# One convolution tap moved from VectorE to ScalarE and GpSimd, and the quarters of a block inverse stored by chunk in PSUM

## The chip, the cores and the metric

The kernel runs on one core of one Trainium2 chip. The metric is the device time of that core in microseconds (us); lower is better. The core has a matrix engine (TensorE, "PE" in the profile; its weight loads are "PEld"), a vector engine (VectorE, "DVE"), an engine for activations (ScalarE, "ACT"), a general engine (GpSimd, "POOL") and one that issues most of the DMAs (SyncE, "SP"). Each runs its own instruction stream in order and waits for the others by semaphores. Operands lie in SBUF; matmul results lie in PSUM.

## The reference, cut to what matters

A decoder of two layers on 16 sequences of 256 tokens of width 256. The change lies in the attention of layer 1, a gated delta rule with 16 query heads and 4 key/value heads of 128:

```python
x = x + _L0_attn_ref(_layernorm(x), ...)      # softmax attention
x = x + _L0_ffn_ref(_layernorm(x), ...)       # mixture of 8 experts
x = x + _L1_attn_ref(_layernorm(x), ...)      # below
x = x + _L1_ffn_ref(_layernorm(x), ...)       # gated MLP

def _L1_attn_ref(x, qkv_w, g_w, b_w, gk_w, conv_w, out_norm_w, o_w):
    qkv = x @ qkv_w.T
    y = sum(conv_w[:, i] * xp[:, i:i + S, :] for i in range(4))   # causal, per channel; xp: qkv, 3 zeros ahead
    qkv = silu(y)
    q, k, v = split(qkv)                     # q, k scaled to unit length
    alpha = exp(log_sigmoid(x @ gk_w.T) / 16); beta = sigmoid(x @ b_w.T)
    def step(St, inp):
        q_t, k_t, v_t, a_t, b_t = inp
        St = St * a_t
        delta = (v_t - k_t @ St) * b_t
        St = St + outer(k_t, delta)
        return St, q_t @ St
    o = scan(step, 0, ...)
    o = rmsnorm(o) * out_norm_w * silu(x @ g_w.T)
    return o @ o_w.T
```

The kernel does the recurrence in chunks of 128 tokens: inside a chunk it needs the inverse of a triangular 128x128 matrix (identity plus a strictly triangular part) for each head.

## The kernel before, in words

Three phases follow one another: layer 0 (attention and experts), attention 1 (the function `gated_delta`), and the last MLP (`ffn`). In attention 1 a **step** is one group of 4 query heads with its key/value head (j) on 512 tokens (s), that is two sequences; there are 4 x 8 = 32 steps. A **unit** is one sequence of a step, two chunks (c = 0, 1) of 128 tokens for 4 heads; there are 64 units. Four generators make the work, and `weave` interleaves them by fixed due times; a scheduler then sets each engine's order ahead of the run.

- `project`, once a step, for six tiles (k, v and four q): six matmuls into a PSUM bank (L902), then the convolution. ScalarE writes the tap without a shift into `acc` (L913). VectorE adds the other three, each a scalar_tensor_tensor that reads the PSUM bank shifted by d and `acc` (L917). ScalarE applies silu (L926), and for q a square (L929) whose sums TensorE makes (L951).
- `decays`, once a unit: for each chunk a DMA brings decays, repeated over all partitions, into `Dm` (L978); VectorE runs a scan over it (L984) with `bI`, which GpSimd makes (L982). `Dm0` has 4 buffers, `Dm1` 5. They stay in use until `back` has read them (o0, L1157, for chunk 0; o1, L1175, for chunk 1).
- `front`, once a unit, makes the inverse. GpSimd fills `XT` with a scaled identity (L996) and makes the triangular matrix `Tf` (L1008), which is split in two fp16 parts `Th` and `Tl`. VectorE puts the first off-diagonal entries into `XT` with copy_predicated (L1013) and transposes (L1019). Then the blocks double: at each of five levels (2, 4, 8, 16, 32) TensorE makes Y from `Th` and `X` (L1027), ScalarE copies it (L1029), TensorE makes Z from `XT` and Y (L1033), and VectorE copies Z under a mask into `X` (L1035) and transposes `X` to `XT` (L1041). The two chunks of `X` alternate element by element, and before the change so do those of Z in its bank.
- `back`, once a unit, solves with the inverse for both chunks (`solve`, z at L1110), carries the state `S0` (L1154), scales the output `O` (L1123, after a power on GpSimd, L88), gates it (L1131, L1133, L1134) and adds the projected rows to x (L1141, L1143).

The loads of `Dm`, of the activations `xT` and of the next weights all go through SP's queue, in order.

Of the kernel before, what the change touches and what calls it, by code (L numbers as in the profile page):

```python
# [10 lines left out]
F32 = mybir.dt.float32  # L11
I32 = mybir.dt.int32
U8 = mybir.dt.uint8
# [4 lines left out]
ALU = mybir.AluOpType  # L18
# [4 lines left out]
P = 128  # L23
# [11 lines left out]
G = H1 // KV1  # L35
LEVELS = (2, 4, 8, 16, 32)
XS = 2.0**12
WS, NS, OS, HS = 2.0**13, 2.0**10, 20.0, 0.5
PS0_BUFS = {"s": 3, "m": 3, "e": 1, "y": 1}
PS0_ROLE = {"s": "s", "t": "s", "p": "m", "n": "s", "v": "m", "o": "m", "r": "s", "e": "e", "y": "y", "l": "m", "g": "m"}  # L40
# [812 lines left out]
def gated_delta(tc, ctx, a, x, ident, identh, ones, psum, made, ws, weights, rsqrt_):  # L853
# [36 lines left out]
    DVE.tensor_scalar(nident, ident, -XS, None, ALU.mult)  # L890
    masks = p.tile([P, 512], F32, tag="Tf", name="masks", bufs=2)[:, :384].rearrange("p (n e) -> p n e", n=6)
    nc.sync.dma_start(out=masks, in_=a["blocks"])
    masks8 = wp.tile([P, 6, 64, 2], U8, tag="masks8", name="masks8")
    for c in range(2):
        DVE.tensor_copy(masks8[:, :, :, c], masks)
    pair1, odd = masks8[:, 0], {s: masks8[:, n + 1] for n, s in enumerate(LEVELS)}
    def three(ps, w, wcols, xs, xcols, flip=False):

        todo = [(c, m, n) for c in range(2) for m, n in ((0, 0), (0, 1), (1, 0))]
# [4 lines left out]
    def project(s, j, xT, w, r):  # L904

        nm = f"{s}_{j}"
        eq = p.tile([P, 4, G], F32, tag="eq", name=f"eq_{nm}", bufs=3)
        raw, tags = {}, cycle(("pr", "bk") if s == j == 0 else ("pr",))
        for n, ct in (("k", G), ("v", G + 1)) + tuple((h, h) for h in range(G)):
            ps = bank(f"pr_{nm}_{n}", next(tags))  # L910
            three(ps, w["wqkv"], slice(ct * P, (ct + 1) * P), xT, slice(0, 512))
            acc = p.tile([P, 512], F32, tag="acc", name=f"acc_{nm}_{n}", bufs=2)
            ACT.activation(acc, ps, AF.Copy, scale=w["cv"][:, ct, 3:4])  # L913
            to, frm = acc.rearrange("p (b t) -> p b t", b=2), ps.rearrange("p (b t) -> p b t", b=2)
            yield
            for d in (1, 2, 3):
                DVE.scalar_tensor_tensor(to[:, :, d:], frm[:, :, : S - d], w["cv"][:, ct, 3 - d : 4 - d], to[:, :, d:], ALU.mult, ALU.add)  # L917
                yield
            if n in ("k", "v"):
                raw[n] = dst = acc  # L920
            else:
                if n == 0:
                    q = p.tile([P, G, 512], F32, tag="q", name=f"q_{nm}")
                    r.update(q=q)
                dst = q[:, n, :]
            ACT.activation(dst, acc, AF.Silu)  # L926
            if n not in ("k", "v"):
                q2 = p.tile([P, 512], F32, tag="q2", name=f"q2_{nm}_{n}", bufs=1)
                ACT.activation(q2, dst, AF.Square)  # L929
            yield  # L930
            if n == "k":

                pk = bank(f"pk_{nm}", "pr").rearrange("p (i d) -> p i d", i=4)
                for i in range(4):
                    PE.transpose(pk[:, i, :], raw["k"][:, i * P : (i + 1) * P], ident)
                ss = p.tile([P, 4], F32, tag="kss", name=f"kss_{nm}")
                k2 = p.tile([P, P], F32, tag="sq", name=f"k2_{nm}", bufs=1)
                for i in range(4):
                    ACT.activation(k2, pk[:, i, :], AF.Square, accum_out=ss[:, i : i + 1])
                DVE.tensor_scalar(ss, ss, 1e-6, None, ALU.add)  # L940
                rsqrt_(ss, 4)
                k = p.tile([P, 4, P], F32, tag="k", name=f"k_{nm}")
                for i in range(4):
                    ACT.activation(k[:, i, :], pk[:, i, :], AF.Copy, scale=ss[:, i : i + 1])
                r.update(k=k)
                yield
            elif n != "v":

                pq = bank(f"pq_{nm}_{n}", "pr")[:, :4]
                for i in range(4):  # L950
                    PE.matmul(pq[:, i : i + 1], lhsT=q2[:, i * P : (i + 1) * P], rhs=ones[:, 0:1], start=True, stop=True)  # L951
                DVE.tensor_scalar(eq[:, :, n], pq, 1e-6, w["sv"][:, 1:2], ALU.add, ALU.mult)  # L952
                yield
            else:
                pv = bank(f"pv_{nm}", "pr")
                for i in range(4):
                    PE.transpose(pv[:, i * P : (i + 1) * P], raw["v"][:, i * P : (i + 1) * P], ident)
                v = p.tile([P, 4, P], F32, tag="v", name=f"v_{nm}", bufs=3)
                ACT.activation(v.rearrange("p i d -> p (i d)"), pv, AF.Copy, scale=w["sv"][:, 0:1])  # L959
                vh = p.tile([P, 2, P], F16, tag="vh", name=f"vh_{nm}", bufs=3)  # L960
                DVE.tensor_copy(vh, v.rearrange("p (b c) d -> p b c d", c=2)[:, :, 0, :])
                pt = bank(f"kn_{nm}", "pr")
                for i in range(4):
                    PE.transpose(pt[:, i * P : (i + 1) * P], r["k"][:, i, :], ident)
                kT = p.tile([P, 512], F32, tag="kT", name=f"kT_{nm}")
                ACT.copy(kT, pt)
                r.update(v=v, vh=vh, kT=kT)
                yield
        r.update(eq=eq)
        yield  # L970

    def decays(s, j, b, r):


        nm, hs = f"{s}_{j}_{b}", slice(G * j, G * j + G)
        Dm = [p.tile([P, G, P], F32, tag=f"Dm{c}", name=f"Dm{c}_{nm}", bufs=4 + c) for c in range(2)]
        for c in range(2):
            nc.sync.dma_start(out=Dm[c], in_=bcast(al_d[4 * s + 2 * b + c, hs, :], 0, P))  # L978
        yield
        for c in range(2):  # L980
            bI = p.tile([P, G, P], F32, tag="bI", name=f"bI_{nm}_{c}")
            POOL.tensor_tensor(bI, bcast(ident, 1, G), bcast(beta[:, 4 * s + 2 * b + c, hs], 2, P), ALU.mult)  # L982
            flat = lambda t: t.rearrange("p h t -> p (h t)")
            DVE.tensor_tensor_scan(flat(Dm[c]), flat(Dm[c]), flat(bI), 0.0, ALU.mult, ALU.add)  # L984
            yield
        end = p.tile([P, G], F32, tag="end", name=f"end_{nm}", bufs=5)
        DVE.tensor_copy(end, Dm[0][:, :, P - 1])
        r.update(A=Dm, end=end)
        yield

    def front(s, j, b, pr, r):
# [1 line left out]

        nm, A = f"{s}_{j}_{b}", r["A"]
        XT = p.tile([P, G, P, 2], F16, tag="XT", name=f"XT_{nm}", bufs=4)
        POOL.tensor_copy(XT.rearrange("p h t c -> p h (t c)").bitcast(I32), bcast(x0.rearrange("p t c -> p (t c)").bitcast(I32), 1, G))  # L996
        cols = lambda c: slice((2 * b + c) * P, (2 * b + c + 1) * P)
        pk = bank(f"kk_{nm}", "fr")[:, : 2 * P].rearrange("p (c t) -> p c t", c=2)
        for c in range(2):
# [10 lines left out]
            POOL.tensor_tensor(Tl[c], Tf, Th[c], ALU.subtract)  # L1010
            yield
        for c in range(2):
            DVE.copy_predicated(  # L1013
                XT.rearrange("p h (n two) c -> p h n two c", two=2)[:, :, :, 1, c], bcast(pair1[:, :, 0], 1, G),
                Th[c].rearrange("p h (n two) -> p h n two", two=2)[:, :, :, 1],
            )
        X = p.tile([P, G, P, 2], F16, tag="X", name=f"X_{nm}")
        words = lambda t: t.rearrange("p h t c -> p (h t c)").bitcast(F32)
        DVE.transpose(words(X), words(XT))  # L1019
# [1 line left out]
        for s_ in LEVELS:  # L1021
            even = lambda t: t.rearrange("p h (n two e) c -> p h n two e c", two=2, e=s_)[:, :, :, 0]
            py = bank(f"Y_{nm}_{s_}", "fr").rearrange("p (c h n) -> p c h n", c=2, h=G)
            pz = bank(f"Z_{nm}_{s_}", "fr").rearrange("p (h n c) -> p h n c", c=2, h=G)
            for c in range(2):
                for h in range(G):
                    PE.matmul(py[:, c, h, :], lhsT=Th[c][:, h, :], rhs=even(X)[:, h, :, :, c], start=True, stop=True)  # L1027
# [2 lines left out]
            yield  # L1030
            for c in range(2):
                for h in range(G):
                    PE.matmul(pz[:, h, :, c], lhsT=XT[:, h, :, c], rhs=Y[:, c, h, :], start=True, stop=True)  # L1033
            split = lambda t: t.rearrange("p h (n e) c -> p h n (e c)", e=s_)
            DVE.copy_predicated(  # L1035
                even(X).rearrange("p h n e c -> p h n (e c)"),
                bcast(odd[s_].rearrange("p (n e) c -> p n (e c)", e=s_), 1, G), split(pz),
            )
            yield
            if s_ < 32:  # L1040
# [31 lines left out]
    def back(s, j, b, pr, xT, w, r):  # L1072
# [20 lines left out]
        def solve(c, rh, rf):  # L1093
# [12 lines left out]
            yield  # L1106
            dz = ps(f"dz{c}")
            per_head(lambda h: PE.matmul(dz[:, h, :], lhsT=XF[:, c, h, :], rhs=res[:, h, :], start=True, stop=True))
            z = half(f"z{c}")
            DVE.scalar_tensor_tensor(z, dz, 1.0 / XS, zh, ALU.mult, ALU.add)  # L1110
            yield
            return z
# [4 lines left out]
        def finish(c, o):  # L1117

            per_head(lambda h: ACT.activation(sq, o[:, h, :], AF.Square, accum_out=f[:, c, h : h + 1]))
            DVE.scalar_tensor_tensor(f[:, c], f[:, c], 1.0 / DK, pr["eq"][:, 2 * b + c, :], ALU.mult, ALU.add)  # L1120
            rsqrt_(f[:, c], G)
            O = half(f"O{c}")
            per_head(lambda h: ACT.activation(O[:, h, :], o[:, h, :], AF.Copy, scale=f[:, c, h : h + 1]))  # L1123
            yield
            return O
# [24 lines left out]
        z0 = yield from solve(0, lambda h: pr["vh"][:, b, :], bcast(v[:, 2 * b, :], 1, G))  # L1150
        st = ps("st")
        per_head(lambda h: PE.matmul(st[:, h, :], lhsT=kb[:, h, :], rhs=z0[:, h, :], start=True, stop=True))
        S0 = half("S0", bufs=2)
        ACT.copy(S0, st)  # L1154
        yield
        o0 = ps("o0")
# [144 lines left out]
```

## Time and profile before

| | us |
|---|---|
| median of 3 runs (3420.18 to 3423.67) | 3420.84 |
| the profiled execution, its time | 3428.7 |
| the profiled execution, its span | 3426.8 |
| attention 1 within the span, about | 1170 to 3195 |

| engine | busy, us | share of the span |
|---|---|---|
| PE | 2963.0 | 86% |
| PEld | 2358.8 | 69% |
| DVE | 2580.1 | 75% |
| ACT | 2157.1 | 63% |
| POOL | 1891.2 | 55% |

The page of the profile has these parts: busy time of each engine; the same in 40 slices of the span; DMA queues; the chain of waits that ended last, followed back from the last instruction; groups of instructions by line (busy us, mean ns of one, then the idle time of the engine just before them and what ended it). Further answers of the trace give one line's instructions (least, median and greatest duration), who waited for whom, busy times in a stretch, and the instructions in order of time. "L917" is line 917 of the kernel before. Ends of matmuls in the trace are modelled, so what one matmul occupies is read from the start of the next.

### The profile page before, as it was taken

Reading aid. Unit: us, or ns where it says so; the run is one execution under the profiler, and the core shown is the slowest. Engines: PE = TensorE matmul, PEld = TensorE weight load, DVE = VectorE, ACT = ScalarE, POOL = GpSimd, SP = SyncE. Lnnn points to the kernel's source line nnn. Section 1 sums busy time; section 2 is a strip of 40 time slices with the busy share of each in tenths; the row PEclk is TensorE's granted clock in tenths of the full one; section 3 lists DMA queues with packets and bytes.
Section 4 is the critical chain, followed back from the end, with each engine's and each line's share of the span. In section 5 each row is a group of like instructions: output and inputs, shape, how many; then the busy total and the mean of one; then the engine's idle time right before and its main releaser. Section 6 shows DMA issues by size and latency. Waiting matters only on the chain.

```text
span 3426.8 us, 76022 instructions
## 1 busy us (share of the span) xinstructions
PE 2963.0 (86%) x29836; PEld 2358.8 (69%) x29836; DVE 2580.1 (75%) x4957; ACT 2157.1 (63%) x5327; POOL 1891.2 (55%) x1763
## 2 busy tenths in 40 slices
PE   4487997988788579899999989999899999999799
PEld 3365775766666357777777777777777777777588
DVE  4677787777775578888788888888888888886422
ACT  2466676666666457767676676766676767676432
POOL 2476876766667445555555555554555555554332
PEclk7699998999999779999999999999999999999899
DMA  6422332322321301211111111111111111110100
GB/s 183 144 77 62 95 86 78 101 73 79 80 52 43 78 16 37 60 46 42 32 35 56 44 44 41 35 38 50 48 50 32 38 33 40 35 35 8 32 19 25
DMA packets 175461, 188.70 MB, mean 55 GB/s; under 512 B 20494, under 2 KB 132878, under 8 KB 173374
## 3 DMA queue, kind: packets, MB, share of 16 engines
q1 hardware_dynamic: 165742, 167.07, 17.5%
q10 hardware_dynamic: 9360, 16.79, 1.6%
q8 instruction: 233, 3.82, 0.5%
q14 instruction: 126, 1.03, 0.1%
HBM read 150.14 MB, written 32.02 MB: 53 GB/s over the span
## 4 chain that ended last, share of the span: by engine, by line
PE 34%; DVE 20%; DMA 5%; ACT 5%; issue 2%; POOL 2%; SPq 0%; ACTq 0%; DVEq 0%; POOLq 0%
PE pr L902 5%; DMA Dm<-al_d 5%; DVE acc L917 3%; PE pq L951 3%; PE g L902 3%; DVE Dm L984 3%; DVE X L1035 2%; PE Z L1033 2%; PE fy L829 2%; PE fg L119 2%; PE fu L119 2%; DVE XT L1013 2%; PE Y L1027 2%; PE y L1141 2%; DVE XT L1041 1%
## 5 line engine op out<-in xcount | busy, mean ns | idle before, releaser
L547 POOL TENSOR_TENSOR el<-e,eh 128x512 f16<-128x512 f32 x384 | 444.9, 1170 | 159.7 <-ACT eh L546 122.1
L917 DVE SCALAR_TENSOR_TENSOR acc<-pr,cv,acc 128x510 f32<-128x510 f32 (+2 forms) x384 | 281.4, 734 | 73.7 <-ACT acc L913 69.7
L1008 POOL TENSOR_TENSOR Tf<-Dm,kkm 128x512 f32<-128x512 f32 x128 | 161.7, 1282 | 251.5 <-DVE kkm L1002 243.3
L543 ACT ACTIVATE e<-t 128x512 f32<-128x512 f32 x384 | 232.4, 606 | 105.0 <-PE t L541 67.5
L1035 DVE CAST_PREDICATED X<-masks,Z 128x512 f16<-128x512 uint8 x320 | 220.7, 690 | 70.8 <-PE Z L1033 70.6
L1134 POOL TENSOR_TENSOR gl<-sg,gh 128x512 f16<-128x512 f32 x128 | 158.0, 1235 | 156.3 <-ACT gh L1133 156.0
L546 ACT ACTIVATE eh<-t 128x512 f16<-128x512 f32 x384 | 232.0, 606 | 13.0 <-PE po L558 12.8
L1029 ACT ACTIVATE Y<-Y 128x512 f16<-128x512 f32 x320 | 191.2, 597 | 74.8 <-PE Y L1027 73.5
L984 DVE TENSOR_TENSOR_SCAN Dm<-Dm,bI 128x512 f32<-128x512 f32 x128 | 182.1, 1423 | 62.4 <-DMA Dm<-al_d 60.3
L1033 PE MATMUL Z<-Y,XT 128*128 128x64 f16 x2560 | 207.4, 249 | 23.6 <-ACT Y L1029 18.8
L88 POOL TENSOR_TENSOR f<-f,neghalf 128x4 f32<-128x4 f32 x128 | 149.2, 1166 | 124.9 <-DVE f L1120 122.7
L1033 PEld LDWEIGHTS <-XT 128*128 128x128 f16 x2560 | 175.3, 121 | 53.9 <-issue 31.8
L902 PE MATMUL pr<-xT,wqkv 128*128 128x512 f16 x768 | 209.3, 413 | 2.9 <-ACT v L959 2.8
L982 POOL TENSOR_TENSOR bI<-ident,beta 128x512 f32<-128x512 f32 x128 | 134.1, 1048 | 136.2 <-DVE Dm L984 98.3
L510 DVE TENSOR_REDUCE nm<-s 128x2 f32<-128x512 f32 x256 | 173.1, 682 | 47.3 <-PE s L509 46.4
L902 PEld LDWEIGHTS <-wqkv 128*128 128x128 f16 x1152 | 119.0, 112 | 120.7 <-issue 38.4
L902 PE MATMUL g<-xT,wga 128*128 128x256 f16 x1536 | 198.9, 281 | 1.4 <-DVE eq L952 0.7
L1141 PE MATMUL y<-woa,gh 128*128 128x256 f16 x1024 | 184.7, 277 | 7.7 <-ACT gh L1133 5.5
L1027 PE MATMUL Y<-X,Th 128*128 128x64 f16 x2560 | 145.5, 202 | 43.4 <-DVE X L1035 34.0
L1041 DVE STREAM_TRANSPOSE XT<-X 128x512 f32<-128x512 f32 x256 | 179.8, 702 | 1.9
L539 PE MATMUL t<-Qt,Kt 128*128 128x512 bf16 x384 | 152.2, 402 | 32.3 <-ACT eh L546 15.2
L1027 PEld LDWEIGHTS <-Th 128*128 128x128 f16 x2560 | 125.4, 101 | 67.2 <-issue 57.9
(363 smaller groups left out, 9829.3 us busy)
## 6 DMA issues: line engine op xcount, KB each, us to landing
Dm<-al_d SPq DMA_DIRECT2D x128, 256.0 KB
cb<-cd SPq DMA_DIRECT2D x128, 128.0 KB
dB<-dc_d ACTq DMA_DIRECT2D x64, 256.0 KB
xT<-xd SPq DMA_DIRECT2D x64, 256.0 KB
Qt<-qd SPq DMA_DIRECT2D x32, 408.0 KB
qd<-both SPq DMA_DIRECT2D x32, 192.0 KB
xr_gidx<-ix_gidx SPq DMA_DIRECT2D x34, 160.0 KB
xr_uidx<-ix_uidx SPq DMA_DIRECT2D x34, 160.0 KB
```

The lines of the kernel that those rows point to most:

```text
L543: ACT.activation(e32, ps, AF.Exp, scale=SC0)
L546: ACT.activation(eh[n], ps, AF.Exp, scale=SC0)
L547: POOL.tensor_tensor(el[n], e32, eh[n], ALU.subtract)
L902: PE.matmul(ps, lhsT=r if flip else l, rhs=l if flip else r, start=k == 0, stop=k == len(todo) - 1)
L917: DVE.scalar_tensor_tensor(to[:, :, d:], frm[:, :, : S - d], w["cv"][:, ct, 3 - d : 4 - d], to[:, :, d:], ALU.mult, ALU.add)
L984: DVE.tensor_tensor_scan(flat(Dm[c]), flat(Dm[c]), flat(bI), 0.0, ALU.mult, ALU.add)
L1027: PE.matmul(py[:, c, h, :], lhsT=Th[c][:, h, :], rhs=even(X)[:, h, :, :, c], start=True, stop=True)
L1029: ACT.activation(Y, py, AF.Copy, scale=XS**-2)
L1033: PE.matmul(pz[:, h, :, c], lhsT=XT[:, h, :, c], rhs=Y[:, c, h, :], start=True, stop=True)
L1035: DVE.copy_predicated(even(X).rearrange("p h n e c -> p h n (e c)"), bcast(odd[s_].rearrange("p (n e) c -> p n (e c)", e=s_), 1, G), split ...
L1041: DVE.transpose(words(XT), words(X))
L1141: PE.matmul(py, lhsT=pair[m][:, h, :], rhs=w["wo"][n][:, h, :], start=k == 0, stop=k == len(todo) - 1)
```

## The change

Of the convolution's three shifted taps, the one with d = 1 is no longer added by VectorE: ScalarE writes it, unshifted, into a new tile `tap` (one buffer), and GpSimd adds it with the shift, as the last of the taps. Z is laid out by chunk in its PSUM bank (each chunk's 256 values side by side), the masks are stored by head and no longer by chunk, and the masked copy reads the two chunks from the two halves of the bank. The first off-diagonal entries are put into `XT` by a scalar_tensor_tensor with a constant `pairs` instead of a copy_predicated with a mask, and GpSimd's fill of `XT` writes only the even columns (256 words instead of 512). `Dm0` gets 5 buffers and `Dm1` 6. Of `back`'s tiles, `z` and `O` share one buffer for both chunks, and `S0` has one buffer instead of two.

```diff
+SMALL = 2.0**-40
...
-    masks8 = wp.tile([P, 6, 64, 2], U8, tag="masks8", name="masks8")
-    for c in range(2):
-        DVE.tensor_copy(masks8[:, :, :, c], masks)
-    pair1, odd = masks8[:, 0], {s: masks8[:, n + 1] for n, s in enumerate(LEVELS)}
+    masks8 = wp.tile([P, 5, G, 64], U8, tag="masks8", name="masks8")
+    DVE.tensor_copy(masks8, bcast(masks[:, 1:], 2, G))
+
+    pairs = wp.tile([P, 64], F32, tag="pairs", name="pairs")
+    DVE.scalar_tensor_tensor(pairs, ident.rearrange("p (e two) -> p e two", two=2)[:, :, 1], XS / SMALL, masks[:, 0], ALU.mult, ALU.add)
+    odd = {s: masks8[:, n] for n, s in enumerate(LEVELS)}
...
             ACT.activation(acc, ps, AF.Copy, scale=w["cv"][:, ct, 3:4])
-            to, frm = acc.rearrange("p (b t) -> p b t", b=2), ps.rearrange("p (b t) -> p b t", b=2)
-            yield
-            for d in (1, 2, 3):
+            tap = p.tile([P, 512], F32, tag="tap", name=f"tap_{nm}_{n}", bufs=1)
+            ACT.activation(tap, ps, AF.Copy, scale=w["cv"][:, ct, 2:3])
+            to, frm, late = (t.rearrange("p (b t) -> p b t", b=2) for t in (acc, ps, tap))
+            yield
+            for d in (2, 3):
                 DVE.scalar_tensor_tensor(to[:, :, d:], frm[:, :, : S - d], w["cv"][:, ct, 3 - d : 4 - d], to[:, :, d:], ALU.mult, ALU.add)
                 yield
+            POOL.tensor_tensor(to[:, :, 1:], to[:, :, 1:], late[:, :, : S - 1], ALU.add)
+            yield
...
-        Dm = [p.tile([P, G, P], F32, tag=f"Dm{c}", name=f"Dm{c}_{nm}", bufs=4 + c) for c in range(2)]
+        Dm = [p.tile([P, G, P], F32, tag=f"Dm{c}", name=f"Dm{c}_{nm}", bufs=5 + c) for c in range(2)]
...
-        POOL.tensor_copy(XT.rearrange("p h t c -> p h (t c)").bitcast(I32), bcast(x0.rearrange("p t c -> p (t c)").bitcast(I32), 1, G))
+        even_cols = lambda t: t.bitcast(I32).rearrange("p (m two) -> p m two", two=2)[:, :, 0]
+        POOL.tensor_copy(
+            even_cols(XT.rearrange("p h t c -> p (h t c)")).rearrange("p (h n) -> p h n", h=G), bcast(even_cols(x0.rearrange("p t c -> p (t c)")), 1, G))
...
-            DVE.copy_predicated(
-                XT.rearrange("p h (n two) c -> p h n two c", two=2)[:, :, :, 1, c], bcast(pair1[:, :, 0], 1, G),
-                Th[c].rearrange("p h (n two) -> p h n two", two=2)[:, :, :, 1],
-            )
+            DVE.scalar_tensor_tensor(
+                XT.rearrange("p h (n two) c -> p h n two c", two=2)[:, :, :, 1, c],
+                Th[c].rearrange("p h (n two) -> p h n two", two=2)[:, :, :, 1], SMALL, bcast(pairs, 1, G), ALU.add, ALU.mult)
...
-            pz = bank(f"Z_{nm}_{s_}", "fr").rearrange("p (h n c) -> p h n c", c=2, h=G)
+            pz = bank(f"Z_{nm}_{s_}", "fr").rearrange("p (c h n) -> p c h n", c=2, h=G)
...
-                    PE.matmul(pz[:, h, :, c], lhsT=XT[:, h, :, c], rhs=Y[:, c, h, :], start=True, stop=True)
-            split = lambda t: t.rearrange("p h (n e) c -> p h n (e c)", e=s_)
+                    PE.matmul(pz[:, c, h, :], lhsT=XT[:, h, :, c], rhs=Y[:, c, h, :], start=True, stop=True)
             DVE.copy_predicated(
-                even(X).rearrange("p h n e c -> p h n (e c)"),
-                bcast(odd[s_].rearrange("p (n e) c -> p n (e c)", e=s_), 1, G), split(pz),
+                X.rearrange("p h (n two e) c -> p (h n) two e c", two=2, e=s_)[:, :, 0],
+                bcast(odd[s_].rearrange("p h (n e) -> p (h n) e", e=s_), 3, 2), pz.rearrange("p c h (n e) -> p (h n) e c", e=s_),
             )
...
-            z = half(f"z{c}")
+            z = half("z")
...
-            O = half(f"O{c}")
+            O = half("O")
...
-        S0 = half("S0", bufs=2)
+        S0 = half("S0")
```

## What the change does to the time: a prediction

> **What bounds the kernel now.** I read the busy table first, then the same for a stretch in the middle of attention 1 (1500 to 3100 us), where all of the change lies:
>
> ```profile
> PE 2963.0 (86%) x29836; PEld 2358.8 (69%) x29836; DVE 2580.1 (75%) x4957; ACT 2157.1 (63%) x5327; POOL 1891.2 (55%) x1763
> ```
> ```profile
> 1500.00:3100.00 1600.00, 1469.27 (x14737) 1185.92 (x14736) 1350.69 (x2256) 1117.98 (x3006) 874.90 (x755) 0.97 0.14 41
> ```
>
> In the second row PE is busy 92% (1469 of 1600), DVE 84%, ACT 70%, POOL 55%, at a clock of 0.97. No engine is full; PE and DVE are coupled by short waits in both directions. So I go to the chain of waits, on the page and for the same stretch:
>
> ```profile
> PE 34%; DVE 20%; DMA 5%; ACT 5%; issue 2%; POOL 2%; SPq 0%; ACTq 0%; DVEq 0%; POOLq 0%
> ```
> ```profile
> by line: DMA Dm<-al_d 9.2%; PE pr L902 8.8%; PE pq L951 5.5%; DVE acc L917 5.4%; DVE Dm L984 5.1%; PE g L902 4.9%; DVE X L1035 4.3%; DVE XT L1013 3.7%; PE Z L1033 3.6%; PE Y L1027 3.3%; issue 3.2%; PE y L1141 2.9%; PE o L1157 2.1%; PE pr_k
> ```
>
> The chain is spread over many lines: no single wait sets the end. Three of its entries are what the change edits (acc L917, XT L1013, Z L1033), one is a transfer whose buffers it adds to (Dm). I therefore cost each edit by the part of its work that lies in the chain, not by its busy time. Attention 1's steady part runs from about 1200 to 3125 us, 1.2 times the stretch; results from the stretch are multiplied by 1.2. Layer 0 and the last MLP keep their instructions and their order, and I cost them at nothing.
>
> **1. The tap leaves VectorE.**
>
> ```profile
> L917 DVE SCALAR_TENSOR_TENSOR acc<-pr,cv,acc x384: 691/742/750, 1201.9 to 3114.8; 128x510 f32<-128x510 f32 x64, 128x508 f32<-128x508 f32 x64, 128x506 f32<-128x506 f32 x64
> ACT q L926 <- DVE acc L917: 84.7, 59, 3.4
> ```
>
> These 384 are the q tiles; with k and v there are 576. In the chain they have 5.4% of 1600 = 86 us, with k and v by count 130 us. One of three goes: 43 us, times 1.2: **-52 us**. (In busy time it is 192 x 0.73 = 141 us of DVE.)
>
> **2. copy_predicated becomes a product.** The old one takes 1059 ns in the mean. The nearest row for the new one is a 128x256 scalar_tensor_tensor with two SBUF inputs:
>
> ```profile
> L177 DVE SCALAR_TENSOR_TENSOR woa<-st_g_split,outs,woa x16: 469/697/1483, 921.4 to 2524.3; 128x256 f16<-128x256 f32 x16
> L1013 DVE COPY_PREDICATED XT<-masks,Th x128: 694/1038/1706, 1205.8 to 3121.7; 128x256 f16<-128x256 uint8 x128
> L984 DVE TENSOR_TENSOR_SCAN Dm<-Dm,bI x128: 1173/1224/2271, 1179.1 to 3077.3; 128x512 f32<-128x512 f32 x128
> ```
>
> Its least is 469 ns; the old one's mean is 365 ns above its own least, and I carry most of that excess over: 0.80 us (between 0.47 and 1.06). So 24% of 3.7% of 1600 = 14 us goes, times 1.2: **-17 us** (0 to -40).
>
> **3. Z by chunk.** What eight matmuls occupy is seen where the next one starts:
>
> ```profile
> 2405.87 0.61 PE L1033 MATMUL Z<-Y,XT 128*128 128x64 f16 x8
> 2406.29 0.68 PE L1067 MATMUL qk<-q,kT 128*128 128x512 f32 x1
> 2402.10 0.41 PE L1027 MATMUL Y<-X,Th 128*128 128x64 f16 x8
> 2402.35 0.67 PE L1067 MATMUL qk<-q,kT 128*128 128x512 f32 x1
> ```
>
> Eight Z take 0.42 us, eight Y of the same size 0.25. Z differs in two things: it writes every second fp32 of its bank, and its weights are read with a step of two. The change ends only the first. The trace can't part them by itself, but another operation loads weights with the same step (`X` at L1055, 98 ns a load) no slower than Y's (101 ns at L1027), and the Trainium skill (PSUM — Partial Sum Buffer, Specifications) names the written side: any non-contiguous pattern slows matmuls there. I take the full 0.17 us a batch: 40% of Z's 3.6% of 1600 = 23 us, times 1.2: **-28 us** (0 if it is the weights; 54 us if all 320 batches counted). The masked copy now reads PSUM with a large step. The sum over three parts at L563 also reads PSUM with a step and takes 549 ns for 384 values, the rate of plain rows (690 ns for 512), so I add nothing; one tenth more would be 22 us of DVE, some 6 in the chain.
>
> **4. What ScalarE and GpSimd take on.** ScalarE: 192 x 0.70 (L913's row) = 134 us. Of its 2157 busy us, 5% of 3427 = 171 us, or 8%, are in the chain: **+11 us**. GpSimd: 192 adds of two fp32 tiles, nearest the row of qd, less the halved fill of `XT`, which lies beside other work:
>
> ```profile
> L1149 POOL TENSOR_TENSOR qd<-q,dB x64: 1266/1276/1588, 1222.7 to 3146.5; 128x512 f32<-128x512 f32 x64
> ```
>
> That is 192 x 1.28 = 246 us; POOL's share of the stretch goes from 55% to about 67%. At POOL's own rate in the chain (2% of 3427 against 1891 busy: 3.6%) it costs 9 us; at the convolution's (130 of about 350 us busy: 37%) 91 us. ScalarE's silu waits for the add now, and behind it in ScalarE's queue stand the copies of Y that TensorE needs. I take **+20 us**, near the low end, because in the order of the changed program 8 other ScalarE instructions (median; 10 for k and v) stand between the last write of a tile's tap and its silu, before 6 and 8: two more, some 1.2 us at L913's pace or a little faster, and the add takes only 0.55 us longer than the tap that it replaces.
>
> **A rule against the change.** The Trainium skill (SBUF — State Buffer, Who interferes with whom) says that a VectorE instruction with two SBUF inputs and a GpSimd instruction that reads SBUF block each other for the whole instruction. The rows agree in kind: L917, with one input in PSUM, keeps to 691-750 ns, while the scan (two SBUF inputs) reaches 2271 and L1013 1706. By the rule at its worst each of the 256 scans and products waits for a full add: 256 x 1.28 = 328 us of DVE, and the change loses. By the rows the mean excess over the least is 0.25 us for the scan (1423 - 1173) and 0.365 for L1013; growing with POOL's share (67/55), 128 x (0.25 + 0.365) x 0.22 = 17 us more of DVE, of which 27% is in the chain (20% of 3427 against 2580): **+5 us**. I go by the rows.
>
> **5. One more buffer for each Dm.** The chain's first entry looks as if it went. The wait itself is
>
> ```profile
> DVE Dm L984 <- DMA Dm<-al_d: 60.3, 60, 2.0
> ```
>
> so at most 60 us of DVE idle can go. But in the order of the changed program the scans move one unit ahead too: between VectorE's z of the unit whose buffer is taken and the scan stand 9 and 10 VectorE instructions (medians for Dm0 and Dm1), before 10 and 13. The DMA is again issued just after the release, and lands after the same 3.3 us. I take **0**, between -60 and +60 (Dm1's scans stand nearer their release than before). Past SP's queue, the loads of `xT` now go behind Dm loads of a later unit; these have a unit's time in hand.
>
> **6. Buffers taken away.** In the trace z of the next unit starts at least 0.26 us after the last o1 matmul of this one in every unit, and `S0` at least 2.3 us after: **0**. For `O` a tenth of the units would wait up to 1.4 us: at most 9 us of ACT, under 1 in the chain.
>
> **The sum.** -52 - 17 - 28 + 11 + 20 + 5 = **-61 us**. The profiled execution had 3428.7 us around its span of 3426.8; it becomes 3367.7. It was 7.9 above the median of the runs, so the forecast is **3360 us** (-1.8%). Its own range is 3310 to 3400.
>
> **The rivals.**
>
> *VectorE sets the pace and all its saving counts.* For it: DVE is busy 84% and waits shortest. Then 141 us of taps and 33 of L1013 (128 x 0.26) go, less 17: 3421 - 157 = **3264 us**. Against it: PE is fuller (92%), and of what it does only Z's 54 us go.
>
> *The Dm wait does go.* The forecast less 60: **3300 us**. For it: the chain's largest entry; against it: the order above.
>
> *GpSimd's queue makes the convolution late (slower).* The place: the add at the end of each tile, in a queue that already idles 243 us for kkm and 156 for gh with everything behind it; ScalarE stands still at the silu, and the copies of Y and Z's chain behind it. The price: 1 us more at each of 192 tiles is 192 us; then 3360 + 192 - 20 = **3530 us**. It decides from about 0.42 us a tile (81 us: the 61 gained and the 20 counted). For it: ScalarE already waits for the convolution in 104 of 192 tiles (59, 22 and 23), and an add takes 0.55 us longer than a tap. Against it: the two further instructions between.
>
> *The change doesn't do what it says.* Z's pace comes from its weights: 3360 + 28 = **3388 us**.
>
> **How the numbers follow.** Forecast 42%; VectorE's pace 15%; Dm's wait gone 12%; Z unchanged 10%; GpSimd late 16% (a third of it within 3440); all parts cancel 5%. The range that holds 8 of 10 is 3265 to 3440: it leaves out half of VectorE's pace and two thirds of GpSimd late, some 18%. A measurement of this kernel tells about 0.2% (7 us) from no change. Faster by more than that: 42 + 15 + 12 + 10 and one of the five that cancel, 80%; within 4%; slower 16%.
>
> **What would show it.** Z's mean falls from 249 ns to near Y's 202: step 3. L1013's successor near 0.8 us: step 2. ScalarE's waits for the add stay near the 145 us it had for the convolution: step 4; several hundred would mean the slower rival. The scan's wait for its DMA near 60 us, or above: step 5; near zero: the rival. Scans well above 1.5 us in the mean would mean the rule was right. The prediction is wrong if PE's busy share in the stretch falls although Z gets cheaper.

## The result, and the profile after

The changed kernel takes **3761.15 us** (median of 4 runs, 3753.61 to 3770.96), the kernel before beside it 3420.51 (3416.91 to 3423.67): a ratio of 1.0998, 95% interval 1.097 to 1.1026. It is 10% slower; the forecast was 1.8% faster, and its range ended at 3440.

From the page of the changed kernel, the busy row and the first row of the chain of waits:

```profile
PE 3041.8 (81%) x29836; PEld 2396.1 (64%) x29836; DVE 2528.5 (67%) x4765; ACT 2280.7 (61%) x5519; POOL 2127.9 (57%) x1955
...
PE 35%; DVE 14%; ACT 11%; DMA 6%; POOL 3%; issue 3%; SPq 0%; ACTq 0%; DVEq 0%; POOLq 0%
```

The stretch from 1500 to 3100 us, the same columns as before (busy us and instructions of PE, PEld, DVE, ACT, POOL, then the clock):

```profile
1500.00:3100.00 1600.00, 1304.64 (x12464) 1032.90 (x12463) 1112.15 (x1800) 1031.96 (x2672) 905.35 (x773) 0.90 0.13 36
```

No engine took the loss over. PE fell from 92% to 82% of the stretch, DVE from 84% to 70%, ACT from 70% to 64%. Only POOL rose, from 55% to 57%. Everything is slower and no engine is full: that points to a loop of waits, and not to an engine, as what sets the pace. The clock fell too (0.97 to 0.90), but a lower clock alone would leave PE as large a share of the stretch busy as it was.

The groups that answer to the prediction's rows (page of the changed kernel; busy us, mean ns, idle before and its releaser), and last Z of the kernel before:

```profile
L924 POOL TENSOR_TENSOR acc<-acc,tap 128x510 f32<-128x510 f32 x128 | 168.6, 1317 | 325.8 <-DVE acc L922 229.0
...
L922 DVE SCALAR_TENSOR_TENSOR acc<-pr,cv,acc 128x508 f32<-128x508 f32 (+1 forms) x256 | 188.4, 736 | 104.0 <-ACT tap L918 101.9
L991 DVE TENSOR_TENSOR_SCAN Dm<-Dm,bI 128x512 f32<-128x512 f32 x128 | 185.2, 1447 | 89.8 <-DMA Dm<-al_d 86.1
...
L916 ACT ACTIVATE acc<-pr,cv 128x512 f32<-128x512 f32 x128 | 88.0, 687 | 227.6 <-PE pr L905 224.6
L1041 PE MATMUL Z<-Y,XT 128*128 128x64 f16 x2560 | 136.9, 198 | 103.9 <-ACT Y L1037 101.1
```

```profile
L1033 PE MATMUL Z<-Y,XT 128*128 128x64 f16 x2560 | 207.4, 249 | 23.6 <-ACT Y L1029 18.8
```

Z's mean fell from 249 to 198 ns, as predicted. The add takes 1.3 us, also as predicted. What is new is where engines stand. ScalarE waits 225 us for the projection itself (L916; it was 66 us at L913), and GpSimd 229 us for the taps: the tiles start late. The same in the lists of waits (us in total, times, longest), first of the kernel before, then of the changed one, with the wait that the slower rival had named as its place:

```profile
ACT acc L913 <- PE pr L902: 66.2, 44, 4.1
```

```profile
ACT acc L916 <- PE pr L905: 224.6, 122, 5.0
...
ACT q L933 <- POOL acc L924: 57.3, 31, 3.9
...
ACT acc_v L933 <- POOL acc_v L924: 15.3, 16, 6.2
...
ACT acc_k L933 <- POOL acc_k L924: 8.7, 2, 7.2
```

ScalarE's silu waits only 81 us for the add. Why are the tiles late, then? Follow one q tile before the change in the order of time (start us, duration us, engine, line):

```profile
2409.23 1.46 PE L902 MATMUL pr<-xT,wqkv 128*128 128x512 f16 x6
...
2410.72 0.69 ACT L913 ACTIVATE acc<-pr,cv 128x512 f32<-128x512 f32 x1
2411.44 2.31 DVE L917 SCALAR_TENSOR_TENSOR acc<-pr,cv,acc 128x510 f32<-128x510 f32 x3 [1.41 <-ACT acc L913]
...
2413.85 0.63 ACT L926 ACTIVATE q<-acc 128x512 f32<-128x512 f32 x1 [1.07 <-DVE acc L917]
...
2414.51 0.63 ACT L929 ACTIVATE q<-q 128x512 f32<-128x512 f32 x1
...
2415.56 0.95 PE L951 MATMUL pq<-ones,q 128*128 128x1 f32 x8
...
2416.37 0.81 PE L902 MATMUL pr<-xT,wqkv 128*128 128x512 f16 x3
```

The next tile's `pr` starts when this tile's `pq` is done, and `pq` needs the whole tile: acc, taps, silu, square. So tile follows tile, one at a time (for k and v their transposes, which wait for the silu, stand in `pq`'s place). Now a q tile of the changed kernel:

```profile
2409.52 1.46 PE L905 MATMUL pr<-xT,wqkv 128*128 128x512 f16 x6
...
2411.02 0.69 ACT L916 ACTIVATE acc<-pr,cv 128x512 f32<-128x512 f32 x1 [0.57 <-PE pr L905]
2411.60 0.68 ACT L918 ACTIVATE tap<-pr,cv 128x512 f32<-128x512 f32 x1
2412.40 0.75 DVE L922 SCALAR_TENSOR_TENSOR acc<-pr,cv,acc 128x508 f32<-128x508 f32 x1 [1.98 <-ACT tap L918]
...
2413.98 0.74 DVE L922 SCALAR_TENSOR_TENSOR acc<-pr,cv,acc 128x506 f32<-128x506 f32 x1
...
2416.03 1.56 POOL L924 TENSOR_TENSOR acc<-acc,tap 128x510 f32<-128x510 f32 x1
...
2417.70 0.62 ACT L933 ACTIVATE q<-acc 128x512 f32<-128x512 f32 x1
...
2418.92 0.63 ACT L936 ACTIVATE q<-q 128x512 f32<-128x512 f32 x1
...
2422.95 0.64 PE L1035 MATMUL Y<-X,Th 128*128 128x64 f16 x8 [2.73 <-DVE X L1027]
...
2423.41 0.77 PE L958 MATMUL pq<-ones,q 128*128 128x1 f32 x3
```

Before, `pq` began 6.3 us after `pr`; here 13.9. VectorE's first tap starts only after ScalarE's second product, GpSimd's add waits behind `Tf`, and then `pq` stands in TensorE's queue behind a Y that itself is late.

Averaged over all q tiles that start between 1500 and 3050 us (from the starts and ends in the two traces; us a tile):

| part of the tile | before | after |
|---|---|---|
| projection, to the end of acc | 2.61 | 2.58 |
| until VectorE's first tap starts | 0.49 | 1.15 |
| VectorE's taps, with what stands between them | 3.75 | 1.86 |
| wait for the add, and the add | | 1.76 |
| wait for silu, silu, square | 1.85 | 2.29 |
| until pq starts | 0.54 | 1.83 |
| pq, and until the next pr starts | 0.91 | 1.01 |
| pr to the next pr | 10.16 | 12.47 |

The parts add up to the distance of two projections, and between `pq` and the next `pr` nothing is left (median 0.00 us in both). Over all tiles, k and v too, that distance is 10.23 us before and 12.10 after. There are 192 tiles, and 192 x 1.87 = 359 us, about the loss of 340. Of the 1.83 us ahead of `pq` TensorE is idle for 0.55 and runs other matmuls that stand ahead of it for the rest (0.03 and 0.51 before).

### The profile page after: what moved, and what is told of

Same layout as the page of the kernel before. It is cut to its first block, busy times and chain, and to the rows that moved or that the text cites. A ratio compares the mean times of both kernels' runs of the same rounds, so it can differ in the third digit from the quotient of the medians.

```text
span 3758.9 us, 76421 instructions
## 1 busy us (share of the span) xinstructions
PE 3041.8 (81%) x29836; PEld 2396.1 (64%) x29836; DVE 2528.5 (67%) x4765; ACT 2280.7 (61%) x5519; POOL 2127.9 (57%) x1955
## 4 chain that ended last, share of the span: by engine, by line
PE 35%; DVE 14%; ACT 11%; DMA 6%; POOL 3%; issue 3%; SPq 0%; ACTq 0%; DVEq 0%; POOLq 0%
DMA Dm<-al_d 5%; PE pr L905 5%; PE y L1148 4%; PE pq L958 3%; DVE Dm L991 2%; PE qk L1074 2%; DVE XT L1022 2%; PE fy L830 2%; PE fg L120 2%; PE fu L120 2%; DVE X L1042 2%; PE g L905 2%; PE Y L1035 1%; DVE acc L922 1%; ACT O L1130 1%
## 5 line engine op out<-in xcount | busy, mean ns | idle before, releaser
L924 POOL TENSOR_TENSOR acc<-acc,tap 128x510 f32<-128x510 f32 x128 | 168.6, 1317 | 325.8 <-DVE acc L922 229.0
L1035 PE MATMUL Y<-X,Th 128*128 128x64 f16 x2560 | 156.7, 208 | 126.6 <-DVE X L1042 64.7
L922 DVE SCALAR_TENSOR_TENSOR acc<-pr,cv,acc 128x508 f32<-128x508 f32 (+1 forms) x256 | 188.4, 736 | 104.0 <-ACT tap L918 101.9
L991 DVE TENSOR_TENSOR_SCAN Dm<-Dm,bI 128x512 f32<-128x512 f32 x128 | 185.2, 1447 | 89.8 <-DMA Dm<-al_d 86.1
L1148 PE MATMUL y<-woa,gh 128*128 128x256 f16 x1024 | 212.7, 304 | 40.4 <-ACT gh L1140 38.6
L1035 PEld LDWEIGHTS <-Th 128*128 128x128 f16 x2560 | 135.2, 105 | 154.6 <-issue 142.0
L905 PE MATMUL pr<-xT,wqkv 128*128 128x512 f16 x768 | 230.7, 446 | 0.3 <-ACT v L966 0.3
L916 ACT ACTIVATE acc<-pr,cv 128x512 f32<-128x512 f32 x128 | 88.0, 687 | 227.6 <-PE pr L905 224.6
L1041 PE MATMUL Z<-Y,XT 128*128 128x64 f16 x2560 | 136.9, 198 | 103.9 <-ACT Y L1037 101.1
L1041 PEld LDWEIGHTS <-XT 128*128 128x128 f16 x2560 | 126.2, 102 | 136.5 <-issue 118.4
L1019 POOL TENSOR_TENSOR Tl<-Tf,Th 128x512 f16<-128x512 f32 x128 | 186.3, 1469 | 2.2 <-ACT Th L1018 2.2
```

The lines of the kernel that those rows point to most:

```text
L905: PE.matmul(ps, lhsT=r if flip else l, rhs=l if flip else r, start=k == 0, stop=k == len(todo) - 1)
L1041: PE.matmul(pz[:, c, h, :], lhsT=XT[:, h, :, c], rhs=Y[:, c, h, :], start=True, stop=True)
L1148: PE.matmul(py, lhsT=pair[m][:, h, :], rhs=w["wo"][n][:, h, :], start=k == 0, stop=k == len(todo) - 1)
```

## The experiments

Of e1 to e12 there is one run each, beside one run of the kernel before on the same chip; of e13 to e15 there are 4, 10 and 6, and the median is given. "Distance" is the mean time from one tile's `pr` to the next in the same stretch, "all tiles" runs from the first `pr` to the last.

| run | us | before beside it | distance, us | all tiles, us |
|---|---|---|---|---|
| before | 3420.5 | | 10.23 | 1932 |
| after | 3761.2 | 3420.5 | 12.10 | 2275 |
| e1_quarters_only | 3412.1 | 3430.8 | 10.06 | 1918 |
| e2_tap_only | 3770.7 | 3430.8 | 11.99 | 2281 |
| e3_all_but_shared_buffers | 3704.2 | 3430.8 | 11.64 | 2219 |
| e4_all_but_tap | 3385.7 | 3430.8 | 9.94 | 1894 |
| e5_add_on_vector | 3630.8 | 3425.8 | 11.14 | 2131 |
| e6_tap_made_by_vector | 3857.5 | 3425.8 | 12.43 | 2362 |
| e7_before_program_order | 3598.1 | 3425.8 | 10.78 | 2041 |
| e8_tap_program_order | 3824.6 | 3425.8 | 12.14 | 2272 |
| e9_before_norm_later | 3436.8 | 3430.9 | 10.18 | 1931 |
| e10_tap_norm_later | 3443.7 | 3430.9 | 10.31 | 1940 |
| e11_copy_ahead_of_silu | 3684.6 | 3430.9 | 11.52 | 2193 |
| e12_copy_after_square | 3403.5 | 3430.9 | 10.10 | 1921 |
| e13_after_norm_later | 3471.1 | 3422.2 | 10.56 | 1965 |
| e14_all_but_tap_norm_later | 3419.0 | 3422.2 | 10.04 | 1914 |
| e15_all_but_tap_timed | 3373.0 | 3426.8 | 9.86 | 1885 |

### Which part of the change loses

e1 keeps the tap on VectorE and the old buffers, and makes only Z by chunk, the product and the halved fill. e2 is the kernel before with only the tap's swap (and one buffer for `S0`, which makes room for `tap`). e3 is the changed kernel with the old buffers of `Dm`, `z` and `O`. e4 is the changed kernel with

```diff
-            tap = p.tile([P, 512], F32, tag="tap", name=f"tap_{nm}_{n}", bufs=1)
-            ACT.activation(tap, ps, AF.Copy, scale=w["cv"][:, ct, 2:3])
...
-            for d in (2, 3):
+            for d in (1, 2, 3):
...
-            POOL.tensor_tensor(to[:, :, 1:], to[:, :, 1:], late[:, :, : S - 1], ALU.add)
```

Expected of e1:

> The kernel before with the quarters by chunk, the product in place of copy_predicated and the halved fill, but three taps on VectorE and the old buffers. Theory T (the tap: GpSimd's add and ScalarE's second copy delay the queues): all of the loss is the tap's, so this one is at or below the kernel before, 3330 to 3420 us. Theory B (the shared buffers of z and O tie the two chunks and neighbouring units together): also 3330 to 3420. Theory Q (the new layout or the product itself costs): 3600 us or more.

Of e2:

> The kernel before with the tap alone moved to ScalarE and GpSimd (S0 has one buffer, so that the new tile fits). Theory T: 3650 to 3800 us. Theory B and theory Q: within 2% of the kernel before, 3350 to 3490.

Of e3:

> The changed kernel with z and O in two buffers each again and Dm in 4 and 5 (S0 still one). Theory B: falls back to 3350 to 3450 us. Theory T: stays at 3700 or more. Theory Q: stays at 3700 or more.

Of e4:

> The changed kernel with all three taps on VectorE again, its shared buffers and its Dm buffers kept. Theory T: 3330 to 3450 us. Theory B: 3650 or more. Theory Q: 3600 or more. If both this one and the one with the old buffers stay slow, tap and buffers each cost by themselves; if both are fast, they cost only together.

The tap alone costs +340 us (e2), the whole loss. Without it the change gains 45 (e4), and Z with the product and the halved fill alone 19 (e1). The buffers matter second: with the old ones the changed kernel is 57 us faster (e3, one run).

### Which half of the tap

Both halves were put on VectorE in turn, in e2's kernel:

```diff
-            POOL.tensor_tensor(to[:, :, 1:], to[:, :, 1:], late[:, :, : S - 1], ALU.add)
+            DVE.tensor_tensor(to[:, :, 1:], to[:, :, 1:], late[:, :, : S - 1], ALU.add)
```

> The tap-only kernel, but VectorE adds the tap that ScalarE has written, so GpSimd has no part in the convolution. Theory P (the add in GpSimd's queue is what costs): 3400 to 3500 us, near the kernel before. Theory A (the second copy out of PSUM on ScalarE, and the waits at it): stays at 3650 or more. Theory O (any change of the convolution makes the planner lay out a worse order): 3550 or more.

```diff
-            ACT.activation(tap, ps, AF.Copy, scale=w["cv"][:, ct, 2:3])
+            DVE.tensor_scalar(tap, ps, w["cv"][:, ct, 2:3], None, ALU.mult)
```

> The tap-only kernel, but VectorE writes the tap from PSUM and GpSimd adds it, so ScalarE has no part beyond what it did before. Theory P: 3650 us or more, as with the tap from ScalarE. Theory A: 3400 to 3500. Theory O: 3550 or more.

Neither half is innocent: with GpSimd out of it (e5) the loss is still 205 us, and with ScalarE out of it (e6) it grows to 432. An explanation by one engine's load can't hold both. What the kernels share is that each puts one link more between `pr` and `pq`. GpSimd's hop is a part of the loss all the same: without it 205 us are left of 340.

### Whether the planned order is to blame

The scheduler that sets the engines' order in advance was left out, in the kernel before and in e2's:

```diff
-    with tile.TileContext(nc, schedule_with_timeline_sim=True) as tc:
+    with tile.TileContext(nc) as tc:
```

> The kernel before with each engine's instructions in the order in which the generators are woven, without the planner that reorders them. No theory gives its time; 3450 to 4200 us. It is the base for the next one.

> The tap-only kernel in the woven order. Theory O (the loss comes from the planner's order): within 2% of the kernel before in the woven order. Theories P and A (the tap itself, wherever the order comes from): 5% or more above it.

In the order in which the program emits its work, the tap still costs 227 us. The planned order makes it worse, but isn't the cause.

### Opening the series

Theory L (for loop: the series of tiles sets the pace) came out of the tiles' times above. The test is to break the loop and keep every instruction: `pq` of tile n is emitted behind the projection of tile n+1, and into a bank of another group, because `pr` has two banks, which `pr` and `pq` shared. Order and bank change together here; that the order was the closer link is read from the 0.00 us between `pq` and the next `pr`. The transposes of k and v stay where they were.

```diff
+        def norm(n, q2):
+            pq = bank(f"pq_{nm}_{n}", "bk")[:, :4]
+            for i in range(4):
+                PE.matmul(pq[:, i : i + 1], lhsT=q2[:, i * P : (i + 1) * P], rhs=ones[:, 0:1], start=True, stop=True)
+            DVE.tensor_scalar(eq[:, :, n], pq, 1e-6, w["sv"][:, 1:2], ALU.add, ALU.mult)
...
             three(ps, w["wqkv"], slice(ct * P, (ct + 1) * P), xT, slice(0, 512))
+            if late:
+                norm(*late)
...
-                pq = bank(f"pq_{nm}_{n}", "pr")[:, :4]
...
+                late = (n, q2)
...
+        norm(*late)
```

> The kernel before, with one move on TensorE: the four small matmuls that sum q's squares (pq of tile n) are emitted after the six projection matmuls of tile n+1, into another PSUM bank, instead of ahead of them. Theory L (the 192 projection tiles run one behind the other, because pr of tile n+1 stands directly behind pq of tile n in TensorE's queue, and pq waits for that tile's taps, silu and square): faster. 128 of 192 tiles lose silu, square and pq from the series, about 3.3 us of 10.2; TensorE is 92% busy in the stretch, so it stops the gain near 100 us: 3290 to 3390 us. Rival W (the loss is the engines' work, and the order on TensorE matters little): 3400 to 3440 us.

> The kernel before with the tap made by ScalarE and added by GpSimd (as e2_tap_only, 3771 us), and with the same move of pq behind the next tile's projection. Theory L: the tap lengthens a tile's latency, and that no longer holds TensorE, so most of the 340 us go: within 100 us of e9_before_norm_later, 3300 to 3480 us. Rival W (GpSimd's adds and ScalarE's products crowd those engines or slow VectorE): the tap still costs 250 us or more over e9_before_norm_later.

With the series open the tap costs 7 us instead of 340. The stretch and three waits of e10:

```profile
1500.00:3100.00 1600.00, 1459.10 (x14624) 1177.02 (x14622) 1283.00 (x2073) 1186.83 (x3140) 1069.66 (x903) 0.98 0.13 40
```

```profile
ACT q L939 <- POOL acc L930: 98.7, 83, 2.8
...
ACT acc_k L939 <- POOL acc_k L930: 49.4, 27, 2.4
...
ACT acc L922 <- PE pr L902: 21.3, 20, 3.1
```

PE is back at 91%, and the wait for the projection fell to 21 us (187 in e2). The silu waits more for the add than in the changed kernel, 156 us with v's 8.0, and nothing is lost by it: a q tile now takes 18.9 us from `pr` to the end of `pq`, but the next `pr` starts 6.5 us after it in the mean. Only q's tiles overlap: from the `pr` of k to the next it is 17.7 us and from that of v 18.5 (8.2 and 12.6 before), and a step of six tiles takes 62 us (61 before).

The other half of L's expectation failed: e9 is no faster than the kernel before. Its stretch:

```profile
1500.00:3100.00 1600.00, 1470.72 (x14712) 1197.67 (x14710) 1346.60 (x2251) 1125.11 (x2998) 877.44 (x756) 0.97 0.13 41
```

PE is 92% busy, as it was (1469.27), and the tiles still come every 10.2 us, though `pq` now ends 18.0 us after its `pr`. So something else holds nearly the same pace: lengthening the series costs at once, and opening it alone finds no gain. What that is stays open. TensorE's work with its short gaps is the first candidate (1469 us for the 156 tiles that fit into 1600 us at 10.23: 9.4 us a tile), but e14 below has less of that work and isn't faster. Others are the turns of k and v, which are still closed (the next `pr` stands right behind their transposes in e9 and e10 too), and a price of the move itself.

**The clock** is a rival that no run tests alone. Where the series is longer, the granted clock in the stretch is lower (0.93 in e2, 0.95 in e11 below, 0.97 before) and TensorE's busy time in the whole kernel is longer, with the same matmuls: 3060.4 us in e2 and 3030.7 in e11, 2963.0 before. So beside e2's loss of 340 us, TensorE spends 97 us more on the same matmuls (their ends are modelled, so this is rough). In e10 the clock is 0.98 and the busy time 2966.3, with the tap still on ScalarE and GpSimd. The lower clock thus goes with the late tiles and not with the tap's work. How much of the loss it makes wasn't parted.

### One copy, inside the series and outside

The same ScalarE copy of each tile (it takes 0.60 to 0.62 us) was added to the kernel before in two places. In both `S0` has one buffer, which makes room.

```diff
+            copy = p.tile([P, 512], F32, tag="copy", name=f"copy_{nm}_{n}", bufs=1)
+            ACT.copy(copy, acc)
-            ACT.activation(dst, acc, AF.Silu)
+            ACT.activation(dst, copy, AF.Silu)
```

> The kernel before plus one ScalarE copy of each projected tile (128 x 512, 192 in all) standing ahead of the silu, which reads the copy. Theory L: the copy's 0.7 us is in the series 192 times, +135 us: 3530 to 3590 us. Rival W (ScalarE is 61% busy, its share of the chain of waits about a tenth): +10 to +30 us, and the same as e12_copy_after_square.

In e12 `ACT.copy(copy, dst)` stands behind the square instead:

> The same 192 ScalarE copies, but each behind the tile's silu and square, where no matmul waits for it. Theory L: ScalarE does the same work, but it stands outside the series: 0 to +50 us, 3420 to 3470 us. Rival W: the same time as e11_copy_ahead_of_silu.

Ahead of the silu it costs 254 us, behind the square nothing (27 us less than the kernel before beside it, one run of each; beside e13 to e15 the kernel before ran from 3402 to 3439 us). The two kernels' copies:

```profile
L927 ACT COPY copy<-acc x128: 601/619/687, 1202.7 to 3375.9; 128x512 f32<-128x512 f32 x128
```

```profile
L931 ACT COPY copy<-q x128: 600/603/651, 1195.9 to 3093.8; 128x512 f32<-128x512 f32 x128
```

Equal work, equal durations (the 128 q tiles are shown), and 281 us between them: only the place differs. L's size was too small: 0.62 us each cost 1.3 us a tile. In e11's tiles the way from the last tap to the silu grew by 1.20 us (the copy, its waits and what the queue put between), silu and square by 0.33, `pq`'s wait by 0.41, and VectorE's taps shrank by 0.59. A late tile also makes the other streams' work, woven between, late. How that share splits wasn't tried.

### The whole change with the series open, and without the tap

> The whole changed kernel, 3761 us, with pq of each tile moved behind the next tile's projection. Theory L (the changed kernel's loss is the longer series of tiles and nothing else): the loss of 340 us goes, and what Z by chunk saves stays, 3380 to 3440 us, not slower than the kernel before by 1%. Rival B (the buffers that the change takes away, and the crowding of GpSimd, keep a part of the loss): 3480 us or more, and a period of the tiles well above 10 us.

> The changed kernel without the tap (e4_all_but_tap, 3386 us in one look), with pq moved. Theory L: once the series is open TensorE's own work sets the pace (it was 92% busy in the stretch before and after the move), and Z's cheaper matmuls come off it: 3330 to 3400 us. If the move costs something of its own (a third user of the back's banks), 3400 to 3440 us.

> The kernel of e4_all_but_tap (3386 us in one look), timed in rounds: the changed kernel with its three taps on VectorE again. The prediction's steps 2 and 3 (the masked copy that became a product, -17, and Z by chunk, -28) sum to -45 us: 3360 to 3390 us. Theory L (the series of tiles sets the pace, so Z's cheaper matmuls shorten the time only where a tile waits for them): 3380 to 3415 us. Rival N (the order that the planner happens to weave moves a kernel by 20 us or more either way, and the parts save nothing that can be told): 3405 to 3440 us.

The changed kernel with `pq` moved (e13) takes 3471 us, a ratio of 1.0129 (1.0091 to 1.0167) to the kernel before: 290 of 340 us are gone. That is above L's 3380 to 3440 and just below rival B's 3480, so "the longer series and nothing else" is not confirmed for the whole change. Against e14, which differs from it by the tap alone, the tap still costs 52 us, where in e10 against e9, with the old buffers but for `S0`, it cost 7. PE is at 89% in e13's stretch, so some wait is left; which isn't settled.

Without the tap, the moved `pq` brings nothing: e14 is at 0.9986 (0.9965 to 1.0007) of the kernel before. L's expectation that Z's saving shows once the series is open failed there. Its stretch has PE at 90%:

```profile
1500.00:3100.00 1600.00, 1440.84 (x14918) 1158.25 (x14916) 1361.19 (x2279) 1132.54 (x3037) 858.24 (x759) 0.97 0.13 40
```

The fastest is e15, the change without its tap and with `pq` where it was: **3373 us, 0.985 (0.9813 to 0.9887)**, faster than both kernels. That lies in the range of the prediction's steps 2 and 3 (3360 to 3390) and below L's 3380 to 3415. It is also 46 us less than e14, which differs by the moved `pq` alone: in this kernel the move has a price of its own, and its cause wasn't tried. Its busy row:

```profile
PE 2895.0 (86%) x29836; PEld 2301.1 (68%) x29836; DVE 2570.5 (76%) x4957; ACT 2163.8 (64%) x5327; POOL 1873.7 (56%) x1763
```

PE has 68 us less to do than before (2963.0) and the tiles come every 9.86 us.

## Why the prediction was wrong

**The step that failed** is the first one, the reading of the chain: "The chain is spread over many lines: no single wait sets the end. ... I therefore cost each edit by the part of its work that lies in the chain, not by its busy time." A loop was hidden in that spread: `pr`, acc, taps, silu, square, `pq` and the next `pr`, 192 times, with other work in the gaps. The chain's entries PE pr L902, PE pq L951 and DVE acc L917, at 8.8, 5.5 and 5.4%, are links of it. In such a loop an added link counts on every turn and not by a share of 8 or 37% of its time; in e11 it cost even twice its own length. The runs show it: the tap's swap takes a tile from 10.23 to 11.99 us and costs 340 us (e2), and 7 us once `pq` stands behind the next projection (e10 against e9). A look at what stands ahead of `pr` in TensorE's order would have shown the loop.

**Step 1**, the tap leaves VectorE, -52: VectorE's part of a q tile did shrink, by 1.89 us, more than the 0.73 of one tap. But the tap came back in the same series.

**Step 4**, +11 and +20: the step mis-sized. Its durations were right (0.69 us for ScalarE's product, 1.32 for the add). It charged ScalarE's product at 8% of its time, because it saw it as load. In a q tile it pushes VectorE's first tap back by 0.66 us: in none of the 192 tiles does that tap start before the product's end (0.12 us after it in the median, 0.23 for q), though it doesn't read it. The add with its wait is 1.76 us of the series, and waits behind it (silu, square, `pq`) grew by 1.7. Taken together, as the swap of e2, the terms -52 + 11 + 20 = -21 measured +340.

**The slower rival**, given 16%, had the right arithmetic, 192 times the lateness of a tile, and the wrong place: ScalarE at the silu. The changed kernel waits 81 us there, less than the 145 expected even if nothing went wrong; e10 waits 156 at no loss. What came late was `pq` on TensorE, and with it the next tile. GpSimd's queue had a part in it: the add waits 0.45 us of its 1.76. The rival's price of 1 us a tile was 1.87.

**Step 2**, the product, -17: wrong. It takes 1201 ns in the mean in the changed kernel and 1062 in e15, the old one 1059; its least is 708, not the 469 of the row it was costed by. Nothing was gained here.

```profile
L1022 DVE SCALAR_TENSOR_TENSOR XT<-Th,pairs x128: 708/1128/1862, 1202.1 to 3445.5; 128x256 f16<-128x256 f16 x128
```

**Step 3**, Z by chunk: right in its cause. Z's mean is 198 ns and Y's 203 to 208, and only the written side was changed, as the rule of the Trainium skill (PSUM — Partial Sum Buffer, Specifications) has it; the weights are still read with a step. In time, e15 gains 54 us on the kernel before beside it, where steps 2 and 3 had 45. That the two sizes are near each other is in part luck, since step 2 gained nothing; how much of the 54 is Z, and how much the buffers or the order, wasn't parted: e1, with the old buffers, gained 19 in one run.

**The rule against the change**, +5: the rows were nearer than the rule's worst. The scan's mean went from 1423 to 1447 ns with GpSimd's adds beside it; at the worst it would have been some 1.28 us longer each. Against e15, the same kernel without those adds, the scan takes 98 ns more (1349) and the product 139: 128 of each make 30 us of VectorE, where the rows gave 17 and the worst case 328.

**Step 5**, `Dm`: the scan's wait for its transfer went from 60 to 86 us, and to 37.5 in e15, inside the -60 to +60 given. **Step 6**, buffers taken away, 0: by one run, wrong by some 57 us where the tiles are late (e3, which undoes steps 5 and 6 together but for `S0`; the two weren't parted).

**"The prediction is wrong if PE's busy share in the stretch falls although Z gets cheaper"**: it fell from 92% to 82%, while Z's mean fell by 51 ns.

## What to carry to other kernels

When every engine is busy and none is full, look for a loop that closes through an engine's order: take one repeated instruction (here the projection), see what stands directly ahead of it in its queue, and follow back what that waits for. If the way leads to the last turn of the same instruction, every microsecond added on it counts as often as the loop turns, and work taken off an engine counts only as far as the way gets shorter. Moving work from a fuller engine to emptier ones can put links into that way. Then open the loop first, or leave the work where it is; here leaving it was better (3373 us in e15, against 3471 with the loop open and the tap moved, e13).

## What the runs showed of the hardware

- A matmul that writes every second fp32 of its bank: Z at 249 ns in the mean, 198 when it writes side by side; its weight loads went from 121 to 102 ns in the mean though their reading didn't change.
- A scalar_tensor_tensor on 128x256 fp16 with a step in its operands took 708 ns at the least, no less than the copy_predicated (694) that it replaced, against 469 for a plain 128x256 one.
- GpSimd at 67% of the stretch beside VectorE (e10: 1069.66 of 1600; 55% in e9) cost no time that can be told (7 us, one run each).
- The granted clock in the stretch was 0.90 where PE was 82% busy (changed kernel), 0.93 at 82% (e2), 0.95 at 84% (e11) and 0.97 to 0.98 at 91 to 92% (before, e9, e10).
